# Router logits of a mixture-of-experts layer computed with tokens as rows instead of experts as rows

## Chip, cores and metric

The kernel runs on one core of one Trainium2 chip. The metric is the device time of one execution in microseconds (us), as the median of repeated runs. Beside it stands a profile of one execution: busy times, waits and the order of instructions on each engine (TensorE is PE, with its weight loads shown apart as PEld; VectorE is DVE, ScalarE is ACT, GpSimd is POOL, SyncE is SP, which issues the DMAs).

## What is computed

The input is 4 sequences of 1024 tokens with 128 features. Three layers with residual connections follow one another: a mixture of experts, a selective state-space layer (Mamba), and the same mixture of experts again.

```python
x = x + 0.5 * ffn(layernorm(x))
x = x + mamba(layernorm(x))
x = x + 0.5 * ffn(layernorm(x))

def ffn(x):                                   # 8 experts, all of them for all tokens
    router_probs = softmax(x @ w_router)      # [tokens, 8]
    gate_weights = softmax((x @ w_gating) / 0.1)
    h = silu(x @ w_gate[e]) * (x @ w_up[e])   # for each expert e, 128 -> 512
    expert_out[e] = h @ w_down[e]             # 512 -> 128
    cw = router_probs * gate_weights
    cw = cw / (cw.sum(-1) + 1e-9)
    return sum(expert_out[e] * cw[e])

def mamba(x):                                 # inner size 256, state size 16
    xs, z = split(x @ W_in)
    xc = silu(causal_conv4(xs) + conv_b)
    dt, B, C = split(xc @ W_x); dt = softplus(dt @ W_dt + b_dt)
    h_t = exp(dt_t * A) * h_(t-1) + dt_t * xc_t * B_t
    y_t = h_t . C_t + xc_t * D
    return (y * silu(z)) @ W_out
```

## The kernel before

**Blocks and stages.** The 4096 tokens are cut into 8 blocks of 512. `order` holds 16 mixture stages: (1, k) is the first mixture of block k, (2, k) the second. In between stands the Mamba part of each block. TensorE runs the stages one after another without a break: for each of the 8 experts of a stage, `gate_part` and `up_part` make two 128x1024 products each, and `down` brings the result back to 128 features. Everything else, the Mamba blocks among it, is threaded between these products.

**Splitting.** The wide products work on a high and a low part: a value is rounded to the faster type `float32r` (`xh`, `wh`) and the remainder is kept in a second tile (`xl`, `wl`). A product is then the sum of three: high x high, high x low, low x high (L641 to L643). The router weights are treated in the same way: `wrg` holds the 8 columns of `w_router` and the 8 of `w_gating`, 16 in all, padded with zeros to 128; `wrg_h` and `wrg_l` are its parts (L249 to L272).

**The plan.** All engines run in an order written out by the program. The class `Plan` holds a clock for each engine with assumed costs; work for VectorE is put in queues (`put`, with a cost and the time from which it is ready) and taken from them when its engine's assumed clock gets there (`fill`), or at once when something needs it (`need`). ScalarE's side work goes through `act_put` and `act_need`. An item's cost and time only decide its place in the order; on the chip each engine runs its instructions in that order and waits for what they read.

**Slots and events.** Time is counted in slots, 64 for each stage and 8 for each expert. A step such as `tr` or `logits` is an event with a slot and often a condition; `run_events` (L1152) lets a due event stand back while its condition says that its input isn't ready, for up to `wait` slots, 12 as a rule (`WAIT`), and then issues it anyhow. For the mixture stages the slots come from `WHEN` and `LOOSE`, counted from the start of the stage. For Mamba block k they count from `START[k]`, in three chains: `front` (norm, projections, convolution, softplus), `mid` (the 16 states, two at a time: exponentials on ScalarE, product, scans and read-out on VectorE, the sum on GpSimd) and `back` (`gate`, the product with silu(z), and `outproj`, the output projection L1073 and the residual). The chain `back` has a patience of 12 slots, and of 24 for the last block (L1177).

**One shared bank.** Small results in PSUM, TensorE's accumulators, go through a single bank, the tile `misc`: norm transposes, logits, projections and the end of each stage. Whoever wants it first waits until the reader of the one before is through (`plan.reader`).

**The logits.** For each stage, `tr` (L462) makes the transposed and split `xh` and `xl`, features as rows and the 512 tokens as columns. `logits` (L481) then makes three products with the padded router weights as the stationary side and all 512 tokens streamed past, which gives `lt`, logits as rows; ScalarE copies 16 rows of it to `ls` (L490), a tile of the ring `tmp` of three, shared with the copies of the expert results. `logits2` (L492), a second event, turns them back with four small transposes (L497) into `lg`, where tokens are rows and the 16 logits of each of the four groups of 128 tokens are columns. `shift` on VectorE takes the maximum of each softmax (L505) and subtracts it (L506). `burst` makes the exponentials on ScalarE, `cw1` to `cw3` the weights, and `cwt` transposes, stores and spreads them over all partitions by DMA.

Of the kernel before, what the change touches and what calls it, by code (L numbers as in the profile page):

```python
# [8 lines left out]
F32 = mybir.dt.float32  # L9
F32R = mybir.dt.float32r  # L10
AF = mybir.ActivationFunctionType
ALU = mybir.AluOpType
AX = mybir.AxisListType
# [5 lines left out]
BIG = 11  # L19
TMP = 3  # L20
TOL = 0.4
START = (72, 144, 232, 328, 432, 544, 656, 744)
REST = (4, 9, 17, 19, 23, 25, 29, 35, 37)
FRONT = {0: (5, 7, 8, 15, 16, 18, 21, 27, 29)}
ZT = {0: 11}
# [17 lines left out]
CWT0 = 11  # L43
# [5 lines left out]
NEVER = 1e9  # L49
WAIT = 12  # L50
# [122 lines left out]
def tile_macaron_mamba_moe(  # L173
# [20 lines left out]
    V, G, S, T = nc.vector, nc.gpsimd, nc.scalar, nc.tensor  # L194

    NB, L, H = x_in.shape
    E, _, F = w_gate.shape
# [3 lines left out]
    TB = 512  # L201
    J = TB // 128
    NBLK = NB * L // TB
# [3 lines left out]
    NE2 = 2 * E  # L207
    P = 128
# [4 lines left out]
    const = ctx.enter_context(tc.tile_pool(name="const", bufs=1))  # L213
    sb = ctx.enter_context(tc.tile_pool(name="sb", bufs=1))
# [3 lines left out]
    plan = Plan()  # L218
# [4 lines left out]
    def misc(name):  # L223
        if plan.reader in plan.spare:
            plan.act_need(plan.reader)
        plan.need(lambda: plan.reader is None or plan.reader[3])
        plan.wait_bank(name)
        return ps.tile([P, TB], F32, tag="misc", bufs=1, name=name)
# [17 lines left out]
    idle = ps.tile([P, P], F32, tag="pd", bufs=1, name="idle")  # L246
    for i in range(12):
        T.matmul(idle, blank, blank, start=True, stop=True)
    wrg = sb.tile([P, P], F32, tag="tmp", bufs=TMP, name="wrg")  # L249
    V.memset(wrg, 0.0)  # L250

    def load_router():
        nc.sync.dma_start(out=wrg[:, 0:E], in_=w_router)
# [2 lines left out]
    ident = const.tile([P, P], F32, name="ident")  # L256
# [7 lines left out]
    V.memset(over, -1.0 / H)  # L264
    V.memset(eps9, 1e-9)

    wrg_h = const.tile([P, P], F32R, name="wrg_h")
    wrg_l = const.tile([P, P], F32R, name="wrg_l")

    def split_router():  # L270
        V.tensor_copy(wrg_h, wrg)
        V.tensor_tensor(wrg_l, wrg, wrg_h.bitcast(F32), ALU.subtract)  # L272

    wh, wl, wd, raws, cast = {}, {}, {}, {}, {}

# [168 lines left out]
    def ffn_events(s):  # L444
        kind, k = order[s]
        d = ffn[s] = {}
        nm = f"f{kind}_{k}"
# [14 lines left out]
        def tr():  # L462
            pt, at = transposed(d["xn"], nm, plan.act_need(*d["xn_it"]))
            xh = d["xh"] = sb.tile([P, TB], F32R, tag="xh", bufs=2, name=f"xh_{nm}")
            xl = sb.tile([P, TB], F32R, tag="xl", bufs=2, name=f"xl_{nm}")
            S.copy(xh, pt)
            if s == 0:
                S.copy(wh[0][:, 1, :], raws[0][:, 1, :])

            def low():  # L470
                V.tensor_tensor(xl, pt, xh.bitcast(F32), ALU.subtract)
                d["xl"] = xl

            plan.reader = d["low"] = plan.put(low, 0.6, plan.on_act(0.6, at))
            if s == 0:
                plan.run(d["low"])
                split_router()
                raw = raws.pop(0)
                V.tensor_tensor(wl[0][:, 1, :], raw[:, 1, :], wh[0][:, 1, :].bitcast(F32), ALU.subtract)

        def logits():  # L481
            plan.need(lambda: "xl" in d)
            xh, xl = d["xh"], d["xl"]
            lt = misc(f"lt_{nm}")
            T.matmul(lt, wrg_h, xh, start=True, stop=False)
            T.matmul(lt, wrg_h, xl, start=False, stop=False)
            T.matmul(lt, wrg_l, xh, start=False, stop=True)
            ls = d["ls"] = sb.tile([NE2, TB], F32, tag="tmp", bufs=TMP, name=f"ls_{nm}")
            t = plan.on_pe(0.7, d["low"][4])
            plan.reader = d["ls_it"] = plan.act_put(lambda: S.copy(ls, lt[0:NE2, :]), 0.6, t)  # L490

        def logits2():  # L492
            ls = d["ls"]
            ls_at = plan.act_need(d["ls_it"])
            lg = misc(f"lg_{nm}")
            for j in range(J):
                T.transpose(  # L497
                    lg[:, j * NE2 : (j + 1) * NE2], ls[:, j * P : (j + 1) * P], ident[0:NE2, 0:NE2]
                )
            lv = lg[:, 0 : J * NE2].rearrange("p (j s e) -> p j s e", j=J, s=2)  # L500
            mx = sb.tile([P, J, 2], F32, tag="mx", bufs=2, name=f"mx_{nm}")
            ex = sb.tile([P, J, 2, E], F32, tag="ex", bufs=2, name=f"ex_{nm}")

            def shift():
                V.tensor_reduce(mx, lv, AX.X, ALU.max)  # L505
                V.tensor_tensor(  # L506
                    ex, lv, mx.unsqueeze(3).to_broadcast([P, J, 2, E]), ALU.subtract
                )
                d["ex"] = ex

            plan.reader = plan.put(shift, 0.3, plan.on_pe(0.3, ls_at))

        def burst(alone=True):
            if "exp" in d:
                return
            plan.need(lambda: "ex" in d)
            ex = d["ex"]
            S.activation(ex[:, :, 0, :], ex[:, :, 0, :], AF.Exp)
            S.activation(ex[:, :, 1, :], ex[:, :, 1, :], AF.Exp, scale=10.0)
            d["exp"] = ex  # L520
            if s == 1:
                a_neg()
            plan.put(cw1, 0.25, plan.on_act(0.3, 0.0, "exp"))
            if alone and (s == 1 or s > 13) and not plan.lo:
                S.preload_act_table_set("silu_and_others")
                plan.on_act(0.0, 0.0, "silu")
# [41 lines left out]

        free = plan.bank_free
        if s == 0:  # L570
            return [(0, ln), (0, nrm), (0, tr), (1, logits), (3, logits2), (4, burst), (CWT0, cwt, lambda: max(free(), d.get("cw_at", NEVER)))]
        ln_at, nrm_at, tr_at, lg_at, lg2_at, bu_at, cwt_at = WHEN.get(s, LOOSE)
        return [
            (ln_at - (8 if kind == 1 and s > 1 else 0), ln, lambda: 0.0 if kind == 1 or k in mixed else NEVER),
            (nrm_at, nrm, lambda: d.get("nb_at", NEVER)),
            (tr_at, tr, lambda: max(free(), max(i[4] or NEVER for i in d["xn_it"]))),
            (lg_at, logits, lambda: max(free(), d["low"][4] if d["low"][3] else NEVER)),
            (lg2_at, logits2, lambda: max(free(), d["ls_it"][4] or NEVER)),
            (lg2_at + 2, lambda: riders.append(lambda: burst(False)), lambda: 0.0 if "ex" in d else NEVER),
            (bu_at, burst, lambda: 0.0 if slot[0] % 8 == 5 and "ex" in d or "exp" in d else NEVER),  # L580
            (cwt_at, cwt, lambda: max(free(), d.get("cw_at", NEVER))),
# [567 lines left out]
    def add(base, evs, wait=WAIT):  # L1149
        chains.append([(max(0, base + ev[0]), wait, *ev[1:]) for ev in evs])  # L1150
# [15 lines left out]
    for s in range(len(order)):  # L1166
        add(8 * GPS * s, ffn_events(s))
        kind, k = order[s]
        if kind == 1 and k + 1 < NBLK:
            add(8 * GPS * s, [(0 if s == 0 else -12, lambda k=k: load_x(k + 1))])  # L1170
        if s < len(order) - 1:
            add(8 * GPS * (s + 1), [(FENDS.get(s, 16), lambda s=s: ffn_end(s), lambda s=s: max(plan.bank_free(), summed(s)))])
    for k in range(NBLK):
        front, mid, back = mamba_events(k)
        add(START[k], front)
        add(START[k], mid, 99)
        add(START[k], back, 24 if k == NBLK - 1 else WAIT)  # L1177
    for e in range(1, E):
        add(8 * (e - 1), [(WL, lambda e=e: load_expert(e)), (WS, lambda e=e: split_expert(e))])
    add(8 * E, [(-24, load_mamba)])  # L1180
# [59 lines left out]
```

## Time and profile before

| | |
|---|---|
| median of 3 runs | 1266.12 us (1266.01 to 1266.13) |
| the profiled execution | 1265.99 us |
| span of its instructions | 1264.2 us, 14417 instructions |
| TensorE's granted clock | 1.000 |
| L485 to L487, three wide logit products | 16 of each, 395 to 423 ns each in the record |
| L490, copy of the logits on ScalarE | x16, 9.0 us, 560 ns each |
| L497, transposes back | x64, 6.7 us, 213 ns each in the record |
| L505 and L506, maximum and difference on VectorE | x16 each, 215 and 224 ns each |

The span runs from the first to the last instruction of the program; the time of an execution also holds what lies before and behind it. Products on TensorE are pipelined and the ends in their records are modelled, so what one costs in a stream is read from the distance between two starts, not from its record. The chain of waits follows the last instruction back, at each step to what released it, and its shares say which engines set the end. A wait is put down to the instruction that came last.

### The profile page before, as it was taken

The numbers are of one execution on the slowest core, as the hardware profiler recorded it, in microseconds if no ns is written. First come the engines' busy times: TensorE is split into PE (matmuls) and PEld (weight loads), VectorE is DVE, ScalarE is ACT, GpSimd is POOL, SyncE is SP. The second block draws the span as 40 slices with busy tenths as digits, with TensorE's granted clock in tenths as the row PEclk, the third lists the DMA queues.
The fourth block names the chain that finished last, engine by engine and source line by source line (L and its number), as shares of the span: only waits on it lengthen the run. The fifth ranks groups of instructions, "written<-read, shape, count | busy, mean of one in ns | idle before, by whom it ended". The sixth has DMA issues, their size and how long they took to land.

```text
span 1264.2 us, 14417 instructions
## 1 busy us (share of the span) xinstructions
PE 1245.2 (99%) x4800; PEld 862.0 (68%) x4800; DVE 1138.2 (90%) x1286; ACT 921.8 (73%) x1326; POOL 706.1 (56%) x557
## 2 busy tenths in 40 slices
PE   9999999999999999999999999999999999999998
PEld 7776666666666666666666666666666666668787
DVE  6985699999899999999999999999999999998676
ACT  7684887776777768787788778778777776666653
POOL 1022465757568647775676567757775676554400
PEclk9999999999999999999999999999999999999999
DMA  4501333343343433334343353432433433311011
GB/s 147 158 26 34 107 112 86 101 112 82 81 107 97 118 91 95 93 99 110 99 100 96 92 119 84 120 98 82 113 98 79 110 92 109 103 56 42 26 43 25
DMA packets 75386, 115.09 MB, mean 91 GB/s; under 512 B 7472, under 2 KB 23728, under 8 KB 75312
## 3 DMA queue, kind: packets, MB, share of 16 engines
q1 hardware_dynamic: 75312, 114.19, 33.6%
q8 instruction: 37, 0.61, 0.2%
q14 instruction: 37, 0.30, 0.1%
HBM read 109.71 MB, written 4.46 MB: 90 GB/s over the span
## 4 chain that ended last, share of the span: by engine, by line
PE 70%; DVE 16%; ACT 5%; issue 5%; POOL 3%; DMA 1%; SPq 0%; DVEq 0%; ACTq 0%; POOLq 0%
PE pd L722 19%; PE pu L641 7%; PE pg L641 7%; PE pg L643 7%; PE pu L643 7%; PE pu L642 7%; PE pg L642 7%; DVE hb_m L1021 5%; DVE h L657 4%; PE pd L697 3%; DVE hb_m L1015 2%; DVE da_m L1033 2%; PE pd L705 1%; ACT da_m L1002 1%; ACT h L625 1%
## 5 line engine op out<-in xcount | busy, mean ns | idle before, releaser
L722 PE MATMUL pd<-h,wd 128*128 128x512 f32 x824 | 391.6, 592 | 1.2 <-ACT tmp L735 1.2
L657 DVE TENSOR_TENSOR h<-h,pu 128x1024 f32<-128x1024 f32 x256 | 311.1, 1215 | 76.9 <-PE pu L643 52.5
L1036 POOL TENSOR_TENSOR y_m<-y_m,da_m 128x1024 f32<-128x1024 f32 x128 | 310.5, 2426 | 106.5 <-DVE hb_m L1015 103.2
L625 ACT ACTIVATE h<-pg 128x1024 f32<-128x1024 f32 x256 | 262.7, 1026 | 140.2 <-PE pg L643 135.2
L641 PE MATMUL pg<-xh_f,wh 128*128 128x512 f32 x510 | 266.9, 523 | 0.7 <-ACT h L625 0.7
L744 POOL TENSOR_TENSOR tmp<-tmp,cwb 128x512 f32<-128x512 f32 x98 | 129.1, 1318 | 196.6 <-issue 106.2
L722 PEld LDWEIGHTS pd<-h,wd 128*128 128x128 f32 x824 | 153.5, 188 | 107.9 <-issue 89.6
L641 PE MATMUL pu<-xh_f,wh 128*128 128x512 f32 x512 | 205.8, 402 | 5.8 <-DVE h L657 5.6
L643 PE MATMUL pg<-xh_f,wl 128*128 128x512 f32 x510 | 201.1, 394 | 0.8 <-DVE wl L299 0.8
L643 PE MATMUL pu<-xh_f,wl 128*128 128x512 f32 x512 | 200.5, 392 | 0.0
L642 PE MATMUL pu<-xl_f,wh 128*128 128x512 f32 x512 | 199.9, 391 | 0.0
L642 PE MATMUL pg<-xl_f,wh 128*128 128x512 f32 x510 | 199.4, 391 | 0.0
L1015 DVE TENSOR_TENSOR hb_m<-dx_m,bcb_m 128x1024 f32<-128x1024 f32 x128 | 166.4, 1300 | 1.8
L1021 DVE TENSOR_TENSOR_SCAN hb_m<-da_m,st_sb,hb_m 128x512 f32<-128x512 f32 x128 | 164.2, 1283 | 2.3
L1002 ACT ACTIVATE da_m<-dt_m,A_sb 128x512 f32<-128x512 f32 x256 | 164.0, 711 | 0.6
L1021 DVE TENSOR_TENSOR_SCAN hb_m<-da_m,hb_m 128x512 f32<-128x512 f32 x128 | 156.7, 1224 | 2.6
L1033 DVE TENSOR_TENSOR da_m<-hb_m,bcb_m 128x1024 f32<-128x1024 f32 x128 | 155.8, 1217 | 1.5
L641 PEld LDWEIGHTS pg<-xh_f,wh 128*128 128x128 f32 x510 | 96.0, 188 | 64.8 <-issue 27.4
L747 POOL TENSOR_TENSOR acc<-acc,tmp 128x512 f32<-128x512 f32 x98 | 130.3, 1330 | 7.6
L642 PEld LDWEIGHTS pg<-xl_f,wh 128*128 128x128 f32 x510 | 96.3, 189 | 50.6 <-issue 36.5
L641 PEld LDWEIGHTS pu<-xh_f,wh 128*128 128x128 f32 x512 | 96.1, 188 | 35.4 <-DVE h L657 15.8
L643 PEld LDWEIGHTS pg<-xh_f,wl 128*128 128x128 f32 x510 | 95.6, 187 | 23.2 <-DVE wl L299 1.2
(181 smaller groups left out, 1494.7 us busy)
## 6 DMA issues: line engine op xcount, KB each, us to landing
bcb_m<-bc_m SPq DMA_DIRECT2D x128, 512.0 KB
cwb<-cd_f SPq DMA_DIRECT2D x128, 256.0 KB
out_dram<-x SPq DMA_DIRECT2D x13, 256.0 KB
x<-in_L_attn_x_dram SPq DMA_DIRECT2D x8, 256.0 KB
wraw<-in_L_ffn_w_gate_dram SPq DMA_DIRECT2D x8, 256.0 KB
wraw<-in_L_ffn_w_up_dram SPq DMA_DIRECT2D x8, 256.0 KB
wd<-in_L_ffn_w_down_dram SPq DMA_DIRECT2D x8, 256.0 KB
cd_f<-ct_f SPq DMA_DIRECT2D x64, 4.0 KB
```

Source lines behind the costliest of these rows:

```text
L625: S.activation(h, pg, AF.Silu)
L641: T.matmul(o[:, q, :], wh[e][:, i, cols[q]], d["xh"], start=True, stop=False)
L642: T.matmul(o[:, q, :], wh[e][:, i, cols[q]], d["xl"], start=False, stop=False)
L643: T.matmul(o[:, q, :], wl[e][:, i, cols[q]], d["xh"], start=False, stop=True)
L657: V.tensor_tensor(h, h, pu, ALU.mult)
L722: T.matmul(d["pd"], wd[e][:, cols], h[0], start=(f == 0), stop=(f == FC - 1))
L747: it = put(lambda: G_.tensor_tensor(acc, acc, t, ALU.add), 1.25, at)
L1002: S.activation(da[:, i, :], d["dt"][:, i, :], AF.Exp, scale=A_sb[:, i, n : n + 1])
L1015: mul = V.tensor_tensor(hb, d["dx"], bcb[:, 0:1, :].to_broadcast([P, ND, TB]), ALU.mult)
L1021: V.tensor_tensor_scan(hb[:, i, :], da[:, i, :], hb[:, i, :], 0.0 if first else st_sb[:, i, n : n + 1], ALU.mult, ALU.add,)
L1033: V.tensor_tensor(da, hb, bcb[:, 1:2, :].to_broadcast([P, ND, TB]), ALU.mult)
L1036: it = pool_put(lambda: G.tensor_tensor(d["y"], d["y"], da, ALU.add), 2.4, plan.dve)
```

## The change

The stationary side and the streamed side of the logits change places. For each of the four groups of 128 tokens, the slice of `xh` is the stationary side, and the high and low router weights stand side by side as 32 streamed columns, tile `wrg_s`; a second product with the slice of `xl` as the stationary side adds the high weights' 16 columns to the first half. The result has tokens as rows at once. The two halves are added by a reduction on VectorE, which replaces the first read of PSUM; the maximum and the difference then work on SBUF. The event `logits2`, the copy `ls` and the transposes are gone, as is the padding with zeros. The assumed costs are 0.88 on TensorE instead of 0.7 and 0.3, and 0.5 instead of 0.3 for `shift`. The start slots of Mamba blocks 4 to 7 are 8, 8, 16 and 16 earlier, and the chain `back` of every block has a patience of 40 slots.

```diff
--- before.py
+++ after.py
@@ -19,7 +19,7 @@
 BIG = 11
 TMP = 3
 TOL = 0.4
-START = (72, 144, 232, 328, 432, 544, 656, 744)
+START = (72, 144, 232, 328, 424, 536, 640, 728)
 REST = (4, 9, 17, 19, 23, 25, 29, 35, 37)
 FRONT = {0: (5, 7, 8, 15, 16, 18, 21, 27, 29)}
 ZT = {0: 11}
@@ -246,8 +246,7 @@
     idle = ps.tile([P, P], F32, tag="pd", bufs=1, name="idle")
     for i in range(12):
         T.matmul(idle, blank, blank, start=True, stop=True)
-    wrg = sb.tile([P, P], F32, tag="tmp", bufs=TMP, name="wrg")
-    V.memset(wrg, 0.0)
+    wrg = sb.tile([P, NE2], F32, tag="tmp", bufs=TMP, name="wrg")
 
     def load_router():
         nc.sync.dma_start(out=wrg[:, 0:E], in_=w_router)
@@ -264,12 +263,11 @@
     V.memset(over, -1.0 / H)
     V.memset(eps9, 1e-9)
 
-    wrg_h = const.tile([P, P], F32R, name="wrg_h")
-    wrg_l = const.tile([P, P], F32R, name="wrg_l")
+    wrg_s = const.tile([P, 2, NE2], F32R, name="wrg_s")
 
     def split_router():
-        V.tensor_copy(wrg_h, wrg)
-        V.tensor_tensor(wrg_l, wrg, wrg_h.bitcast(F32), ALU.subtract)
+        V.tensor_copy(wrg_s[:, 0, :], wrg)
+        V.tensor_tensor(wrg_s[:, 1, :], wrg, wrg_s[:, 0, :].bitcast(F32), ALU.subtract)
 
     wh, wl, wd, raws, cast = {}, {}, {}, {}, {}
 
@@ -482,33 +480,30 @@
             plan.need(lambda: "xl" in d)
             xh, xl = d["xh"], d["xl"]
             lt = misc(f"lt_{nm}")
-            T.matmul(lt, wrg_h, xh, start=True, stop=False)
-            T.matmul(lt, wrg_h, xl, start=False, stop=False)
-            T.matmul(lt, wrg_l, xh, start=False, stop=True)
-            ls = d["ls"] = sb.tile([NE2, TB], F32, tag="tmp", bufs=TMP, name=f"ls_{nm}")
-            t = plan.on_pe(0.7, d["low"][4])
-            plan.reader = d["ls_it"] = plan.act_put(lambda: S.copy(ls, lt[0:NE2, :]), 0.6, t)
-
-        def logits2():
-            ls = d["ls"]
-            ls_at = plan.act_need(d["ls_it"])
-            lg = misc(f"lg_{nm}")
+            lv = lt[:, 0 : 2 * J * NE2].rearrange("p (j h n) -> p j h n", j=J, h=2)
             for j in range(J):
-                T.transpose(
-                    lg[:, j * NE2 : (j + 1) * NE2], ls[:, j * P : (j + 1) * P], ident[0:NE2, 0:NE2]
+                T.matmul(
+                    lt[:, j * 2 * NE2 : (j + 1) * 2 * NE2], xh[:, j * P : (j + 1) * P],
+                    wrg_s.rearrange("p h n -> p (h n)"), start=True, stop=False,
                 )
-            lv = lg[:, 0 : J * NE2].rearrange("p (j s e) -> p j s e", j=J, s=2)
+                T.matmul(
+                    lt[:, j * 2 * NE2 : j * 2 * NE2 + NE2], xl[:, j * P : (j + 1) * P],
+                    wrg_s[:, 0, :], start=False, stop=True,
+                )
             mx = sb.tile([P, J, 2], F32, tag="mx", bufs=2, name=f"mx_{nm}")
             ex = sb.tile([P, J, 2, E], F32, tag="ex", bufs=2, name=f"ex_{nm}")
 
             def shift():
-                V.tensor_reduce(mx, lv, AX.X, ALU.max)
+                V.tensor_reduce(
+                    ex.rearrange("p j s e -> p j (s e)"), lv.rearrange("p j h n -> p j n h"), AX.X, ALU.add
+                )
+                V.tensor_reduce(mx, ex, AX.X, ALU.max)
                 V.tensor_tensor(
-                    ex, lv, mx.unsqueeze(3).to_broadcast([P, J, 2, E]), ALU.subtract
+                    ex, ex, mx.unsqueeze(3).to_broadcast([P, J, 2, E]), ALU.subtract
                 )
                 d["ex"] = ex
 
-            plan.reader = plan.put(shift, 0.3, plan.on_pe(0.3, ls_at))
+            plan.reader = plan.put(shift, 0.5, plan.on_pe(0.88, d["low"][4]))
 
         def burst(alone=True):
             if "exp" in d:
@@ -568,14 +563,13 @@
 
         free = plan.bank_free
         if s == 0:
-            return [(0, ln), (0, nrm), (0, tr), (1, logits), (3, logits2), (4, burst), (CWT0, cwt, lambda: max(free(), d.get("cw_at", NEVER)))]
+            return [(0, ln), (0, nrm), (0, tr), (1, logits), (4, burst), (CWT0, cwt, lambda: max(free(), d.get("cw_at", NEVER)))]
         ln_at, nrm_at, tr_at, lg_at, lg2_at, bu_at, cwt_at = WHEN.get(s, LOOSE)
         return [
             (ln_at - (8 if kind == 1 and s > 1 else 0), ln, lambda: 0.0 if kind == 1 or k in mixed else NEVER),
             (nrm_at, nrm, lambda: d.get("nb_at", NEVER)),
             (tr_at, tr, lambda: max(free(), max(i[4] or NEVER for i in d["xn_it"]))),
             (lg_at, logits, lambda: max(free(), d["low"][4] if d["low"][3] else NEVER)),
-            (lg2_at, logits2, lambda: max(free(), d["ls_it"][4] or NEVER)),
             (lg2_at + 2, lambda: riders.append(lambda: burst(False)), lambda: 0.0 if "ex" in d else NEVER),
             (bu_at, burst, lambda: 0.0 if slot[0] % 8 == 5 and "ex" in d or "exp" in d else NEVER),
             (cwt_at, cwt, lambda: max(free(), d.get("cw_at", NEVER))),
@@ -1174,7 +1168,7 @@
         front, mid, back = mamba_events(k)
         add(START[k], front)
         add(START[k], mid, 99)
-        add(START[k], back, 24 if k == NBLK - 1 else WAIT)
+        add(START[k], back, 40)
     for e in range(1, E):
         add(8 * (e - 1), [(WL, lambda e=e: load_expert(e)), (WS, lambda e=e: split_expert(e))])
     add(8 * E, [(-24, load_mamba)])
```

## The prediction

> **What bounds the kernel.** I read the page's busy rows and slices first, then the chain of waits, then the waits of TensorE, then the order in time around single logits, and last the groups of instructions with the shapes kept apart.
>
> ```profile
> PE 1245.2 (99%) x4800; PEld 862.0 (68%) x4800; DVE 1138.2 (90%) x1286; ACT 921.8 (73%) x1326; POOL 706.1 (56%) x557
> ...
> PE   9999999999999999999999999999999999999998
> ...
> DVE  6985699999899999999999999999999999998676
> ...
> PE 70%; DVE 16%; ACT 5%; issue 5%; POOL 3%; DMA 1%; SPq 0%; DVEq 0%; ACTq 0%; POOLq 0%
> ```
>
> TensorE is full in all slices but the last, and 70% of the chain that ends last runs through it. A busy PE row alone does not prove that it works at its rate, so I compared starts: in the quiet stretches of the three-product lines (L641 to L643) one 128x512 product follows another after 0.227 us, and the largest groups add up to roughly 1215 us at their own quiet spacing. What is left, about 45 us, is the head (the first product starts at 8.36 us), the tail, and waits. So time taken from TensorE's stream comes off the end nearly one for one. VectorE is the second engine: in the middle stages it stands at 76 or 77 us of 80, with some 3 to 5 us free in each. That its delays do reach TensorE is seen in the waits (columns: us in total, times, longest us):
>
> ```profile
> PE pu L641 <- DVE h L657: 5.6, 11, 0.9
> ...
> PE lt_f L485 <- DVE xl_f L471: 0.8, 2, 0.6
> ...
> PE cwt_f L556 <- POOL cw_f L547: 0.5, 1, 0.5
> ```
>
> **What goes from TensorE.** The logits run 16 times. The three wide products start at 9.86, 10.09 and 10.33 us, and the next line's at 10.56: 0.70 us. The four transposes back are worth a look in the order in time (columns: start, us, engine, line):
>
> ```profile
> 778.02 0.40 PE L643 MATMUL pg<-xh_f,wl 128*128 128x512 f32 x1
> 778.35 0.42 PE L497 MATMUL lg_f<-ident,ls_f 16*128 16x16 f32 x4
> 778.70 0.50 PE L641 MATMUL pu<-xh_f,wh 128*128 128x512 f32 x1
> 779.04 0.40 PE L642 MATMUL pu<-xl_f,wh 128*128 128x512 f32 x1
> ```
>
> From L643 to L642 there are 1.02 us where two ordinary steps would take 0.45, so four transposes of 16 columns cost 0.56 us, with hardly any streaming in them. The product behind them shows 0.50 instead of 0.39: its own weight load, otherwise hidden under the product before, lies open for 0.11. I read 0.56 as five open loads of 0.112, the four of the transposes and the next one. All 16 places give 0.55 to 0.56. Removed: 16 x (0.70 + 0.56) = 20.2 us.
>
> **What comes to TensorE.** Eight pairs of a full 128x128 load (a slice of xh or xl) and a product of 32 or 16 columns. No row shows this form, so bounds: the output projection L1073 runs 16 pairs with full loads in 1.78 us, 0.111 each, giving 0.89; the transposes at 0.56 / 4 = 0.14 a pair give 1.12. Farther off, the load's record is 0.188 long (L485); eight of them one after another would be 1.50, though the open part just seen speaks against it. The transposes are nearest, for they too have nothing to stream under which a load could hide; by their reading I take nine open loads, 9 x 0.112 = 1.01, or 16.1 us in all. Net for TensorE: -4.0 us, with -6.0 (0.89) and -2.3 (1.12) as near ends and +3.9 (1.50) as the far one.
>
> A rule of the Trainium skill speaks against the change: the page "TensorEngine Tiling (Array Packing)", section "When to Use Tiling", would make a streamed side of 64 columns or fewer the stationary one, and here the narrow side becomes the streamed one. The page "TensorE: Matmul & The Clock Gate", section "LDWEIGHTS (loading the stationary operand)", gives columns / 1.2 ns, so by an estimate from it eight loads take 0.85 us and the net would be -6.5 us; the open 0.11 in the trace agrees with that rate, and the first rule overlooks that the narrow stationary form brings transposes with it.
>
> **VectorE.** Three operations instead of two on its in-order queue, ahead of whatever up-product (L657) is behind them; TensorE waits for that through pu. Removed: 0.215 (L505) + 0.224 (L506) = 0.439. Added: a sum over 128 elements. The reduces over 32 and 64 take 0.178 (L540) and 0.212 (L533), 0.034 per 32, so 128 make 0.28; then the maximum from SBUF like L533, 0.212, and the difference, 0.22. Together 0.71, or +0.27 each, +4.4 us in all. The bounds on the path are 0 (the free 3 to 5 us of each stage hide it) and 4.4 (no cover left); I take its share of the chain, 16%, +0.7 us.
>
> **ScalarE and the shared bank.** The copy L490 goes, 16 x 0.56 = 9.0 us of an engine with a quarter free; at its 5% of the chain, -0.4. The single misc bank is taken once instead of twice; of the waits that name it, 0.2 us of L890 on ex and 1.0 us of loads on ls, the loads are partly under products. Bounds for both together are 0 and -1.2; I keep -0.4 and add nothing. The tmp ring of three loses a user, which only loosens it.
>
> **Head.** The memset (0.165) and the split over 128 columns (0.217 + 0.292) shrink to 16 columns. After the split VectorE makes wl, done at 10.10 and first read by L643 at 11.03: 0.9 us of cover, so I book nothing; uncovered it would be at most -0.5. The two DMAs of the router stay in place on SP's queue, and their landing is before the split either way.
>
> **Starts and patience.** A stage of 64 slots takes about 80 us, so 8 and 16 slots are 10 and 20 us: blocks 4 and 5, then 6 and 7, issue everything earlier, their norms, projections, the bc store and its reload on SP's queue, scans, gate and output projection. The scans cannot move that far: their read-outs (L1033) run nearly without a gap from 274 to 1102 us, VectorE being their limit. What does move is the gate and projection at a fixed offset; block 7's read-out ends at 1102 and its projection starts only at 1153, so there is room. The longer wait of 40 slots lets a projection stand back when its product is late; one such stall is seen, 0.43 us beyond the ordinary step in front of L1073 at 404.3, for GpSimd's gate product L1062. I book -0.4 for it and 0 for the earlier starts, with ends of -1.3 (the L485 and L556 waits shown above vanish) and +5.6 (the waits for the up-product double because VectorE's queue is kept fuller).
>
> **Sum.** -4.0 + 0.7 - 0.4 - 0.4 = -4.1 us. The profiled execution took 1265.99 us with a span of 1264.2, 1.8 us lying around it; the median is 1266.12, so the offset is the same: 1262.0 us.
>
> **Rivals.**
> - *Larger gain, 1258.0.* Loads at the L1073 price (-6.0), ScalarE and the projection as above (-0.8), VectorE's extra hidden, both late waits gone (-1.3): -8.1. For it: load and stream overlap there. Against it: that row streams 128 columns to hide under. Chance 0.14.
> - *Nothing that can be measured, 1265.5.* TensorE comes to the up-products sooner and waits there: of the -4.1, 3.5 return as waits on L657 (it already has 5.6). For it: VectorE above 95% in the middle. Against it: 70% of the chain is TensorE. A measurement tells apart about 0.2%, 2.5 us. Chance 0.16.
> - *Slower through VectorE, 1271.3.* Blocks 4 to 7 pressed closer and 4.4 us more reduces use up its free time; up-products come late. All 4.4 on the path, the 5.6 doubled, less 4.0 and 0.8: +5.2. It decides once a middle stage has less free than the 0.27 added plus one displaced 1.2 us operation, against 3 to 5 now. Chance 0.13.
> - *Slower through the loads, 1269.9.* Open loads of 0.188: +3.9 + 0.7 - 0.8 = +3.8. Decides above 0.157 a pair, where eight equal the 1.26 removed. Chance 0.05.
>
> **How the numbers follow.** The forecast has 0.52, its own range 1259.3 to 1263.7 (the -6.0 end with VectorE's part hidden, and the -2.3 end). Faster by over 0.2%: 0.52 + 0.14 = 0.66; within: 0.16; slower: 0.13 + 0.05, 0.18. The range 1257.0 to 1269.0 leaves out the tips of the larger gain and much of the slower cases.
>
> **What would show it.** Eight products of 32 and 16 columns spaced near 0.11 us; the span from the product before to the second after near 1.01 above two steps (0.89 and 1.12 are the ends, 1.50 the fourth rival). A sum of 0.28 us on VectorE, L490 and L497 gone. TensorE's wait on L657 at about 5.6; above 10 the third rival is at work. The projection at 404 without its stall. The forecast is wrong if TensorE's stream is shorter by 4 us and the span is not: then the waits tell where it went.

## The result, and the profile after

The changed kernel is slower: 1274.11 us in the median of 4 runs (1273.98 to 1276.78) against 1266.07 us for the kernel before on the same chip. The ratio is 1.0068, with a 95% interval of 1.0053 to 1.0082, so 8.0 us are lost where 4.1 were forecast to be won. The profiled execution of after is the longest of its four, 1276.78 us with a span of 1274.7; its granted clock is 0.997 because two stretches of 3.4 us, from 8.2 and from 605.5 us, ran at half clock, by estimate some 1.7 us each. The execution of after with a granted clock of 1.000 took 1273.98 us, so the loss of 8.0 us does not need them. The profile is read for places and durations, and the sums below are made from medians, in which a difference of a microsecond can be the clock's.

The busy row, two rows of slices and the chain of the page after:

```profile
PE 1245.5 (98%) x4816; PEld 862.3 (68%) x4816; DVE 1142.6 (90%) x1301; ACT 908.7 (71%) x1306; POOL 703.5 (55%) x557
...
PE   9999999999999999999999999999999999999998
...
DVE  5985599999999999999989999999998999998676
...
PE 14%; DVE 3%; issue 1%; POOL 1%; ACT 0%; DVEq 0%; POOLq 0%
```

TensorE is as busy as before in the record (1245.2) although it has less to do: the record of a product that is held up or runs at half clock is longer, as a row below shows, so the busy row does not show the saving. The chain's shares add up to 19% only: it was followed back through the last fifth of the span and lost there, so it can't be set beside the 70% of before. What helps is the list of TensorE's waits (us in total, times, longest):

```profile
PE pu L635 <- DVE h L651: 7.3, 14, 1.4
PE pg L635 <- ACT h L619: 3.9, 5, 1.4
PE pd L699 <- DVE hl L661: 3.3, 2, 1.7
PE lt_f L485 <- DVE xl_f L469: 1.8, 2, 1.2
PE cwt_f L551 <- POOL cw_f L542: 1.4, 2, 0.9
```

Every one has grown: the up-products' (L635 after L651) from 5.6, the gate products' (L635 after L619) from 0.7, the down-products' (L699) from 1.7, the logits' from 0.8, the transposes' of the weights from 0.5. No single one is as large as the loss, and they lie all over the span. The groups that belong to the change, shapes kept apart (us busy, mean ns of one, idle before):

```profile
L489 PE MATMUL lt_f<-wrg_s,xl_f 128*128 128x16 f32 x64 | 15.0, 258 | 0.0
L485 PE MATMUL lt_f<-wrg_s,xh_f 128*128 128x32 f32 x64 | 14.2, 251 | 2.1 <-DVE xl_f L469 1.8 <-DVE st_sb L1026 0.3
...
L501 DVE TENSOR_TENSOR ex_f<-ex_f,mx_f 128x64 f32<-128x64 f32 x16 | 8.3, 521 | 0.5
L497 DVE TENSOR_REDUCE ex_f<-lt_f 128x64 f32<-128x128 f32 x16 | 4.5, 283 | 3.8 <-PE lt_f L489 3.8
L500 DVE TENSOR_REDUCE mx_f<-ex_f 128x8 f32<-128x64 f32 x16 | 3.5, 220 | 0.6
```

The sum over 128 elements takes 283 ns and the maximum 220, as forecast. The difference does not: 521 ns where L506 took 224. And the new products are cheaper than forecast. Their distances are seen in the order in time (start, us, engine, line; the wait ahead in brackets):

```profile
603.34 0.28 PE L485 MATMUL lt_f<-wrg_s,xh_f 128*128 128x32 f32 x1 [1.19 <-DVE xl_f L469]
603.47 0.26 PE L489 MATMUL lt_f<-wrg_s,xl_f 128*128 128x16 f32 x1
603.58 0.26 PE L485 MATMUL lt_f<-wrg_s,xh_f 128*128 128x32 f32 x1
...
604.14 0.26 PE L489 MATMUL lt_f<-wrg_s,xl_f 128*128 128x16 f32 x1
604.25 0.48 PE L635 MATMUL pu<-xh_f,wh 128*128 128x512 f32 x1
...
605.91 3.37 PE L716 MATMUL pd<-h,wd 128*128 128x512 f32 x4
```

From 603.34 to 604.25 there are 0.91 us for eight pairs: 0.112 each after the first. Measured as the prediction measured the old ones, from the product before to the second after, less two ordinary steps, 10 of the 16 places cost 0.89 to 0.90 us. So TensorE's work went down by 16 times some 0.36 us, about 5.7 us. The last row shows something else: four down-products that take 3.37 us here take 1.88 us elsewhere. The granted clock of the stretch says why (length, then busy us of PE, PEld, DVE, ACT, POOL with counts, granted clock, share of DMA, GB/s):

```profile
606.00:610.00 4.00, 4.00 (x8) 1.55 (x7) 3.83 (x7) 1.08 (x2) 0.57 (x1) 0.64 0.45 113
```

**Where TensorE falls behind.** For every product I took its start less the sum of the quiet steps of all products ahead of it, which is what TensorE has lost so far, and cut each kernel's stream at the same shares of its work. The growth of that loss in us, in profiled executions, by stretches that end near the time named, with some kernels of the experiments below (the last row is e8 of experiment 4):

```
                          300   450   600   750   900  1050  1200   end
before                   15.3   4.2   3.1   4.9   3.9   5.5   4.5   1.1
after                    18.8   5.8   7.4   4.3   7.8   7.1   5.4   1.2
early starts, old logits 16.7   4.2   4.4   7.3  16.5   4.1   3.2   1.2
blocks 4 and 6 earlier   17.0   4.2   4.3   5.6  11.3   3.2   5.9   1.1
blocks 4, 5, 7 earlier   16.8   4.2   4.3   7.3   3.6   3.9  12.0   1.2
new logits, old order    15.5   5.4   3.1   5.7   3.5   5.8   3.9   1.2
```

Before loses 42.5 us in all, after 57.8. The 15.3 more eat the 5.7 won and leave 9.6 of the 10.5 us by which the two profiled spans differ; the other 0.9 lie behind the start of the last product. By estimate up to 3.4 of the 15.3 are the two stretches at half clock. The rest comes in most stretches, so one cause would not do; the experiments take the change apart.

### The profile page after: what moved, and what is told of

Same layout as the page of the kernel before. It is cut to its first block, busy times and chain, and to the rows that moved or that the text cites. A ratio compares the mean times of both kernels' runs of the same rounds, so it can differ in the third digit from the quotient of the medians.

```text
span 1274.7 us, 14444 instructions
## 1 busy us (share of the span) xinstructions
PE 1245.5 (98%) x4816; PEld 862.3 (68%) x4816; DVE 1142.6 (90%) x1301; ACT 908.7 (71%) x1306; POOL 703.5 (55%) x557
## 5 line engine op out<-in xcount | busy, mean ns | idle before, releaser
L651 DVE TENSOR_TENSOR h<-h,pu 128x1024 f32<-128x1024 f32 x256 | 310.8, 1214 | 77.3 <-PE pu L637 53.0
L619 ACT ACTIVATE h<-pg 128x1024 f32<-128x1024 f32 x256 | 262.6, 1026 | 158.3 <-PE pg L637 151.8
L635 PE MATMUL pg<-xh_f,wh 128*128 128x512 f32 x510 | 263.9, 518 | 4.6 <-ACT h L619 3.9
L738 POOL TENSOR_TENSOR tmp<-tmp,cwb 128x512 f32<-128x512 f32 x98 | 131.8, 1345 | 201.7 <-issue 85.1
L635 PE MATMUL pu<-xh_f,wh 128*128 128x512 f32 x512 | 207.1, 404 | 7.8 <-DVE h L651 7.3
L635 PEld LDWEIGHTS pg<-xh_f,wh 128*128 128x128 f32 x510 | 96.0, 188 | 72.0 <-issue 27.3
L635 PEld LDWEIGHTS pu<-xh_f,wh 128*128 128x128 f32 x512 | 96.2, 188 | 39.4 <-DVE h L651 19.8
```

The source lines that it names most:

```text
L619: S.activation(h, pg, AF.Silu)
L635: T.matmul(o[:, q, :], wh[e][:, i, cols[q]], d["xh"], start=True, stop=False)
L651: V.tensor_tensor(h, h, pu, ALU.mult)
L738: it = put(lambda: G_.tensor_tensor(t, t, cwb, ALU.mult), 1.25, at)
```

## The experiments

The kernel before was run with each group: 1266.24, 1265.99, 1266.17 and 1266.15 us. Ratios are to the kernel before in the same group, with the 95% interval; they take in all executions and so differ a little from the quotient of the medians.

**1. The early starts alone.** The logits of before, `START` and patience of the change.

```diff
-START = (72, 144, 232, 328, 432, 544, 656, 744)
+START = (72, 144, 232, 328, 424, 536, 640, 728)
-        add(START[k], back, 24 if k == NBLK - 1 else WAIT)
+        add(START[k], back, 40)
```

> The old logits, with only the earlier starts of blocks 4 to 7 and the patience of 40 slots. Three theories. ORDER: the time goes to a different order of all the work around the logits, which the plan makes from other assumed costs, and not to the logits themselves; then this, which is a reordering too, may land anywhere from 1264 to 1271, with no tie to the 1274 of the change. VECTOR: the added reduction and the slower difference on VectorE make the up-products late; then this has none of it, 1265 to 1267. MOVES: the earlier starts crowd VectorE and ScalarE; then 1271 to 1275 here.

Measured: 1278.97 us, 1.0096 (1.0081 to 1.0112): 12.7 us lost by a part that was booked at nothing. With the old logits the patience moves no instruction, so this is the starts' doing. The profiled execution is the slowest of the four (1281.06 us, granted clock 0.994), 15.1 us above that of before, and the table above puts 12.6 of these between 750 and 900 us, where block 6 begins (slot 640 of 64 slots in 80 us is 800 us). The order in time there:

```profile
818.12 0.69 DVE L806 TENSOR_TENSOR x<-x,fo 128x512 f32<-128x512 f32 x1 [0.54 <-PE fo L798]
...
822.38 0.20 POOL L360 TENSOR_TENSOR nb_m<-nb_m,minus 128x4 f32<-128x4 f32 x1
...
822.61 0.49 ACT L414 ACTIVATE xn_m<-x,nb_m,rs_m 128x128 f32<-128x128 f32 x1 [0.79 <-POOL nb_m L360]
...
824.04 1.28 ACT L1002 ACT_TABLE_LOAD   x1
...
825.33 2.56 ACT L1002 ACTIVATE da_m<-dt_m,A_sb 128x512 f32<-128x512 f32 x4
825.52 0.27 PE L438 MATMUL pt_m<-ident,xn_m 128*128 128x128 f32 x1
...
827.80 1.25 ACT L414 ACTIVATE xn_m<-x,nb_m,rs_m 128x128 f32<-128x128 f32 x3
...
828.33 0.86 PE L438 MATMUL pt_m<-ident,xn_m 128*128 128x128 f32 x2 [2.54 <-ACT xn_m L414]
```

The first mixture of block 6 hands over `x` at 818.12. Its norm for the Mamba block needs VectorE, GpSimd (until 822.58) and ScalarE. ScalarE makes one of four groups of tokens, and then, as its written order has it, a silu, a table load and four exponentials of another block. TensorE has been sent to the transposes at 825.52, does the one that it can, and stands for 2.54 us. The transposes were due while the norm was not done; they are issued after their 12 slots of patience all the same. From 827.8 us, still within the wait, the clock is halved for nearly 7 us:

```profile
826.00:830.00 4.00, 1.67 (x5) 1.17 (x6) 3.90 (x4) 3.44 (x8) 2.54 (x4) 0.73 0.25 51
830.00:834.00 4.00, 4.00 (x11) 3.11 (x10) 3.34 (x4) 2.50 (x3) 1.53 (x1) 0.50 0.35 80
834.00:838.00 4.00, 4.00 (x14) 2.57 (x13) 3.16 (x3) 0.71 (x2) 0.00 (x0) 0.92 0.61 172
```

So a wait of 2.5 us costs about 6, by estimate: itself, and half of 6.8 us at half clock. Two more waits follow in this stretch, 0.97 us at 868.18 (L954, for `xc_m`) and 2.66 us at 878.18 (L975, for `dt_m` on ScalarE), and from 879.0 another 3.4 us at half clock; together that makes some 11 of the 12.6 us. The execution with the highest granted clock, 0.998, still took 1276.89 us, so most of the loss does not need the half clock. The Trainium skill, "TensorE: Matmul & The Clock Gate", section "Part 1: The HAM clock gate (the "warmup" mystery)", has the clock at half rate after at least one idle window of 3.4 us. The lengths seen here, 3.4 and 6.8 us, fit its window. Its rule on when does not: here waits of only 1.2 us (603.34, after) and 2.5 us went ahead of it. The length of a wait does not decide either: a10 (experiment 5) has the same wait of 1.19 us at 600.37 and m46 (experiment 2) one of 2.57 us at 1145.58, both with the clock at 1.00 behind them, and of two nearly equal waits, 1.81 us at 380.83 in e4 (experiment 3) and 1.80 us at 383.03 in e5 (experiment 4), only the second is followed by half clock. What decides stays open; that a wait causes it at all is read from the order of the two and was not tried by itself.

**2. Which blocks.** Two kernels with the old logits and some of the earlier starts, and one with the changed logits (sum left in PSUM, see 4) in which blocks 4 and 7 go back:

```diff
 m46:  START = (72, 144, 232, 328, 424, 544, 640, 744)
 m457: START = (72, 144, 232, 328, 424, 536, 656, 728)
 a11:  START = (72, 144, 232, 328, 432, 536, 640, 744)
```

> The old logits, with blocks 4 and 6 started earlier, 5 and 7 left. BLOCK 6: 1274 to 1280. CROWDING: half of the 12.7 us, 1270 to 1274.

> The old logits, with blocks 4, 5 and 7 started earlier and block 6 left at 656. BLOCK 6 (its norm is now due at slot 637, before slot 649 where the mixture that feeds it hands over, so its steps are issued before their inputs are there): 1265 to 1269. CROWDING (all earlier starts together fill VectorE and ScalarE): 1272 to 1277, some two thirds or more of the 12.7 us of all four.

> The changed kernel with the sum written back to PSUM and the starts of blocks 4 and 7 back at 432 and 744 (blocks 5 and 6 stay earlier; without one of these the plan can't be made). BLOCK 6: it stays, so little is won against 1271.9, 1270 to 1274. CROWDING: 1265 to 1269.

Measured: 1275.68 us (1.0070, 1.0055 to 1.0085), 1276.75 (1.0083, 1.0068 to 1.0098) and 1275.66 (1.0070, 1.0055 to 1.0086). The idea that block 6 alone was too early fell: without it the time is hardly better. The loss only moves: m46 has its 11.3 us at 750 to 900, m457 none there but 12.0 between 1050 and 1200, where block 7's projection meets a gate product that isn't made:

```profile
1150.89 1.07 PE L697 MATMUL pd<-hh,wds 128*128 128x512 f32 x4
1154.48 2.56 PE L1073 MATMUL po_m<-w_out_sb,zs_m 128*128 128x128 f32 x16 [2.52 <-DVE zs_m L1057]
```

The projection takes 2.56 us in the record instead of 2.05: the clock is halved there again (0.59 in the stretch from 1156 to 1160). In before the same steps of block 7, the last read-out, GpSimd's sum, the gate product and the projection, stand so:

```profile
1144.87 1.22 DVE L1033 TENSOR_TENSOR da_m<-hb_m,bcb_m 128x1024 f32<-128x1024 f32 x1
...
1147.45 2.40 POOL L1036 TENSOR_TENSOR y_m<-y_m,da_m 128x1024 f32<-128x1024 f32 x1
...
1151.98 1.21 DVE L1057 TENSOR_TENSOR zs_m<-zs_m,y_m 128x1024 f32<-128x1024 f32 x1
...
1153.25 2.05 PE L1073 MATMUL po_m<-w_out_sb,zs_m 128*128 128x128 f32 x16
```

The projection starts 0.06 us after the gate product ends, and that 7 us after the last read-out, so it can come 16 slots, 20 us, earlier only if the read-outs do. In m457 they do not: the last one starts at 1147.00. In e1, with all four blocks earlier, it starts at 1131.68, and the projection at 1142.42 has no wait. And a11, with two blocks less moved than the same kernel with the full change of starts (a10 in 5, 1271.93), is 3.7 us slower than it, though two of its four executions have a granted clock of 0.994. The starts do not add up block by block.

**3. VectorE's share without the new products.** The old logits in the old order, with a sum-like reduction over 128 elements put ahead (each element taken twice, so the values stay) and the difference made from SBUF:

```diff
-                V.tensor_reduce(mx, lv, AX.X, ALU.max)
+                V.tensor_reduce(
+                    ex.rearrange("p j s e -> p j (s e)"),
+                    lg[:, 0 : J * NE2].rearrange("p (j n) -> p j n", j=J).unsqueeze(3).to_broadcast([P, J, NE2, 2]),
+                    AX.X, ALU.max,
+                )
+                V.tensor_reduce(mx, ex, AX.X, ALU.max)
...
-                    ex, lv, mx.unsqueeze(3).to_broadcast([P, J, 2, E]), ALU.subtract
+                    ex, ex, mx.unsqueeze(3).to_broadcast([P, J, 2, E]), ALU.subtract
```

> The old logits in the old order, but VectorE makes three operations as in the change: a reduction of 128 elements from PSUM (here the maximum of each value with itself), the maximum from SBUF, and the difference with both sides in SBUF, all at the old assumed cost. VECTOR: most of the loss is here, 1270 to 1275. ORDER and MOVES: hidden for the most part, 1266 to 1268.

Measured: 1272.26 us, 1.0051 (1.0034 to 1.0068): 6.0 lost where +0.7 was booked. Two views of it, its group of the difference and TensorE's wait for the up-products, 5.6 us before:

```profile
L511 DVE TENSOR_TENSOR ex_f<-ex_f,mx_f 128x64 f32<-128x64 f32 x16 | 10.8, 673 | 0.5
```

```profile
PE pu L646 <- DVE h L662: 10.2, 14, 1.8
```

The difference took 224 ns from PSUM and takes 673 from SBUF. Why is seen in the order in time of after, where one of them is caught:

```profile
454.14 2.36 POOL L1030 TENSOR_TENSOR y_m<-y_m,da_m 128x1024 f32<-128x1024 f32 x1 [6.86 <-DVE hb_m L1009]
454.55 2.04 DVE L501 TENSOR_TENSOR ex_f<-ex_f,mx_f 128x64 f32<-128x64 f32 x1
...
456.51 1.21 DVE L651 TENSOR_TENSOR h<-h,pu 128x1024 f32<-128x1024 f32 x1
```

An operation of 0.22 us begins 0.41 us after a long addition on GpSimd and ends at 456.59, 0.09 us after that addition. In after 6 of the 16 are stretched so, to 0.44 to 2.04 us, and all six end 0.08 to 0.09 us after a GpSimd operation that had begun before them; the shortest take 0.22. The Trainium skill, "SBUF — State Buffer", section "Who interferes with whom", says that a VectorE instruction with two SBUF inputs and a GpSimd instruction that reads SBUF take one read interface in turn, the later one waiting for the whole of the other. The trace agrees, 2.04 us for 0.22; the prediction did not use it.

**4. The new products in the old order.** Here the new products stand where the transposes were, an empty item keeps the place of the copy in the plan, and all other instructions keep their order. e5 has the change's `shift`; e8 writes the sum back into free columns of the PSUM tile, so that the difference reads PSUM; e6 leaves out the maximum and the difference (the exponentials of the unshifted logits, whose common factor cancels in the quotient).

```diff
 e8 and a10, in shift():
+                sv = lt[:, 2 * J * NE2 : 3 * J * NE2].rearrange("p (j n) -> p j n", j=J)
+                V.tensor_reduce(sv, lv.rearrange("p j h n -> p j n h"), AX.X, ALU.add)
+                hv = sv.rearrange("p j (s e) -> p j s e", s=2)
+                V.tensor_reduce(mx, hv, AX.X, ALU.max)
...
-                    ex, ex, mx.unsqueeze(3).to_broadcast([P, J, 2, E]), ALU.subtract
+                    ex, hv, mx.unsqueeze(3).to_broadcast([P, J, 2, E]), ALU.subtract
```

> The new logits with every assumed cost, event and start of the old kernel, so that all other instructions on all engines stand in the old order; the eight pairs stand where the transposes back stood. ORDER: TensorE's stream is 5.7 us shorter and nothing is shuffled, so 1260 to 1263. VECTOR: the three operations on VectorE cost as much here as in the change, so 1270 to 1275. MOVES: 1260 to 1264.

> The new logits in the old order, but the sum of the two halves is written back to PSUM, so that maximum and difference read PSUM as in the old kernel; still three operations. PORT (the difference with both sides in SBUF waits for GpSimd's long operations, up to 2.1 us a time): 3 to 5 us below the 1268.2 of the new logits in the old order, 1263 to 1265. REDUCTION (any third operation on VectorE costs this much): 1267 to 1269.

> The new logits in the old order, without the maximum and the difference (the factor they stand for cancels in the quotient): one operation on VectorE instead of two in the old kernel. If TensorE's shorter stream (5.7 us) reaches the end when VectorE is not burdened: 1259 to 1262. If TensorE's saving is lost to other waits in any case: 1265 to 1268.

Measured: e5 1268.21 us (1.0015, 1.0005 to 1.0025), e8 1262.43 (0.9976, 0.9964 to 0.9987), e6 1259.07 (0.9943, 0.9928 to 0.9958). The one difference between e5 and e8, the place of the sum, is worth 5.8 us, and 4.8 between their executions at a granted clock of 0.999 or more (1266.96 and 1262.20 in the median). In e8 the difference is back at its length, though 7 of its 16 run beside a GpSimd operation, and the up-products' wait is near that of before:

```profile
L510 DVE TENSOR_TENSOR ex_f<-lt_f,mx_f 128x64 f32<-128x64 f32 x16 | 3.6, 224 | 0.5
```

```profile
PE pu L645 <- DVE h L661: 6.5, 11, 1.3
```

These runs also price VectorE's time. From e8 to e6 it loses 0.289 + 0.224 + 0.224 - 0.279 = 0.458 us a stage, 7.3 in all, and the end comes 3.4 us sooner: 0.46 us for one. From before to e4 it gains 0.282 + 0.220 + 0.673 - 0.439 = 0.736 a stage, 11.8 in all, and the end is 6.0 later: 0.51 for one. Half, not the 16% of the chain. With it e8 is accounted for: -5.7 on TensorE, and 4.8 us more VectorE time at 0.46, +2.2, make -3.5; measured -3.6.

**5. The change with one part undone.** a10 is the change with the sum in PSUM; e2b is the change with the old patience.

> The changed kernel with the sum written back to PSUM, order otherwise as in the change. PORT: 3 to 5 us below 1274.1, 1269 to 1271, and what is left above 1266 is the order with its earlier starts. ORDER alone: 1273 to 1275.

> The changed kernel with the old patience of the chain back (12 slots, 24 for the last block), the earlier starts kept. MOVES, if by the patience: 1265 to 1269. ORDER: another order, 1269 to 1277. VECTOR: as the change, 1273 to 1275.

Measured: a10 1271.93 us (1.0045, 1.0030 to 1.0060), 2.2 below after; e2b 1277.37 (1.0083, 1.0068 to 1.0098), 3.3 above it, and 1.6 above it between the executions at a granted clock of 1.000 (1275.62 and 1273.98). So the patience helps here, by more than was booked. Whether it mends a loss by the early starts was not tried by itself: with the old logits it moves nothing, early starts or not. Even with the sum in PSUM the change is slower than before, so the wait for GpSimd is the smaller part.

**6. The order alone.** The kernel before with one assumed cost changed, 0.5 for `shift` instead of 0.3, which moves instructions in VectorE's order (at least 175 of 1286, by the two traces) and adds no work; and e8 with the same edit.

```diff
-            plan.reader = plan.put(shift, 0.3, plan.on_pe(0.3, ls_at))
+            plan.reader = plan.put(shift, 0.5, plan.on_pe(0.3, ls_at))
```

> The old kernel with nothing changed but one assumed cost in the plan, 0.5 instead of 0.3 for the maximum and difference; the instructions are the same, some hundred stand elsewhere. ORDER: a reordering costs by itself, 1268 to 1275. If the order matters only through the earlier starts: 1265.5 to 1267.5.

> The new logits with the sum in PSUM, in the order that the old kernel takes with an assumed cost of 0.5 for the maximum and difference. If the gains of the two add up: 1262.4 - 1.1, some 1261. If the order's gain belongs to the old instructions: 1262 to 1265.

Measured: n1 1264.88 us (0.9992, 0.9982 to 1.0001) and e8n 1262.16 (0.9966, 0.9955 to 0.9977). Such an edit is worth some 1.1 us in the median with no work changed, though the interval reaches 1, and what it brings to one kernel it does not bring to the next: e8n is within its spread of e8.

**7. The change's own events with the old starts.** In e8 the copy's place was kept. The change makes the logits one event instead of two, and the plan sets all that follows anew. With the change's assumed costs and the old starts the planner finds no order (a norm falls due ahead of the Mamba block it needs), so these four have others. All but p6 have the sum in PSUM.

```diff
 p3 (old starts, old patience), p4 (starts and patience of the change), p6 (as p3, shift as in the change):
-            plan.reader = plan.put(shift, 0.5, plan.on_pe(0.88, d["low"][4]))
+            plan.reader = plan.put(shift, 0.3, plan.on_pe(1.0, d["low"][4]))
 p5 (as p3):
+            plan.reader = plan.put(shift, 0.25, plan.on_pe(0.88, d["low"][4]))
```

> The new logits as one event as in the change, sum in PSUM, but the old starts and the old patience, with 1.0 and 0.3 as assumed costs so that the plan can be made. STARTS (the earlier starts are what the order costs): 1261 to 1265. REST (leaving out the second event and the copy shuffles the order to its harm): 1269 to 1273.

> The same with the early starts and the patience of the change. STARTS: 6 to 12 us above the run with old starts, 1270 to 1276. REST: within 2 us of it.

> Old starts and patience again, with 0.88 and 0.25 as assumed costs, so another order of the same work. STARTS: 1260 to 1266, like the first. If orders differ much among themselves whatever the starts: more than 3 us from the first.

> The logits exactly as in the change, sum and difference in SBUF, with the old starts and patience and 1.0 and 0.3 as assumed costs. If the difference waits for GpSimd here as elsewhere: 2 to 6 us above the run with the sum in PSUM. If the loss of the change is all in the starts: at most 1 us above it.

Measured: p3 1266.89 us (1.0003, 0.9993 to 1.0012), p4 1275.88 (1.0073, 1.0058 to 1.0088), p5 1266.41 (1.0003, 0.9993 to 1.0012), p6 1269.91 (1.0030, 1.0019 to 1.0041). From p3 to p4 only starts and patience differ: 9.0 us. From p3 to p6 only the place of the sum: 3.0. And p3 and p5 agree, some 4 us above e8, but their orders are nearly one: 21 of VectorE's 1301 instructions have to be moved to turn one into the other, against 203 from p3 to e8. So this order around the logits gives back the whole gain of the new products, even without the two other losses. Whether one event instead of two does so as such, or this order is a bad one by chance, was not tried: p4 and a10 differ in nothing but two assumed costs and lie some 4 us apart.

Where the early starts cost time in the changed kernel is seen in the gate products' wait for ScalarE: 0.7 us in p3, 2.5 in p4, 3.8 in a10 and 3.9 in after. The longest in after stands behind four exponentials of a Mamba block:

```profile
881.24 2.56 ACT L996 ACTIVATE da_m<-dt_m,A_sb 128x512 f32<-128x512 f32 x4
...
885.11 1.02 ACT L619 ACTIVATE h<-pg 128x1024 f32<-128x1024 f32 x1
...
886.19 0.50 PE L635 MATMUL pg<-xh_f,wh 128*128 128x512 f32 x1 [1.38 <-ACT h L619]
```

The two waits of experiments 1 and 2 are not met in after: block 6's transposes at 826.26 and block 7's projection at 1163.26 start without one.

**The account.** Nine of the sixteen times (e1, e5, e8, a10, e2b, a11, n1, p3 and p5) fell outside every range expected for them; in e5 and a10 losses that were set against each other as rivals are there together. In medians, from before (1266.1) to after (1274.1):

```
new products, old order, sum in PSUM        1262.4   -3.7
the change's own event and order (p3)       1266.9   +4.5
its starts, patience, assumed costs (a10)   1271.9   +5.0
the difference from SBUF (after)            1274.1   +2.2
```

The steps depend on the order in which they are taken: the starts cost 5.0, 9.0 (p3 to p4) or 12.7 us (e1), the place of the sum 2.2, 3.0 (p6) or 5.8 (e5). Their signs hold in all of them. Between executions at a granted clock of 0.999 or more the four steps are -3.8, +3.8, +5.2 and +2.9 us.

## Why the prediction was wrong

- **TensorE, -4.0 booked, -5.7 measured.** The mechanism and both bounds were right, the choice between them was not. The transposes were taken as the nearest row, with one open load more than there are pairs (1.01 us). The L1073 price, 0.111 a pair, was the right one (0.90 measured): the row with the same full load priced the pair, though it streams 128 columns and not 32 or 16. The fourth rival, with open loads of 0.188, is out.
- **VectorE, +0.7 booked.** Two durations were right to 0.01 us. Two things failed. "I take its share of the chain, 16%": half of what VectorE is given reaches the end (0.46 and 0.51). And "the difference, 0.22" was taken from a row that reads PSUM, though the text says that the new ones work from SBUF. There it waits for GpSimd, 0.52 on average and up to 2.04. By the measured price the 4.4 us alone are +2.2, and the stretching (8.3 - 3.6 us) another 2.3, which agrees with the 2.2 between a10 and after.
- **The early starts, 0 booked, end +5.6.** This is the step with the largest miss: 5 to 13 us. The prediction let the gate and the projection move because "block 7's read-out ends at 1102 and its projection starts only at 1153, so there is room". That is a misreading: in before the last read-out of block 7 ends at 1146.09 and its gate product at 1153.19 (experiment 2), so the projection already started as soon as it could, and could move only with the read-outs. Nor did the prediction ask when the inputs of the other moved steps exist. Their slots run out first: at the norm of block 6 (experiment 1) and the gate product of block 7 (experiment 2) TensorE stands for 2.5 us, where the longest such wait that the prediction found in before was 0.43 us (L1073 at 404 us). These two waits are seen with the old logits (e1, m457). In after the same starts show as gate products that wait for ScalarE, 3.9 us instead of 0.7; the rest of the starts' share there was not traced to single waits. That a late input can be followed by half clock was not seen coming, and no row of before shows it; after loses its 8 us without it, too.
- **Patience, -0.4 booked.** The stall that it was booked for is still there: in after TensorE sits idle for 0.25 us ahead of the same projection at 407.03, in before for 0.27. With the old logits the patience moves nothing; with the change it is worth 3.3 us (1.6 at full clock), in another place.
- **ScalarE, -0.4 booked.** The copies are gone, 9.0 us, and ScalarE's busy time fell by 13.1. A gain of its own was not isolated: e8's sum closes without it.
- **What had no step at all.** One event instead of two changes the plan's clock, and with it the order of work far from the logits, +4.5 us in the one order that was run. The prediction held only the work of an edit against the time, not the new order that the planner writes for the rest. Which of the exchanged instructions matter stays open: p3's loss over e8 lies in several stretches, +2.9 us before 600 and +2.6 before 900 among them, and other stretches win.
- **The rivals.** The third, slower through VectorE at 1271.3, had the sign, and its sentence "Blocks 4 to 7 pressed closer and 4.4 us more reduces" names two of the parts. Its price was built on the up-products' wait doubling, 5.6 to 11; it went to 7.3, and the rest came in the waits of gate products, down-products, logits and weight transposes. That five waits would each grow a little was no case of its own.

## What to carry to other kernels

In a kernel whose whole order is written by a planner, price an edit in three parts: the work, the waits of what is moved (for each moved step, when its last input exists), and the new order of everything else. The last cost 4.5 us here, about as much as the work saved, and is measured by holding the old order and changing the work alone. Where an operand of VectorE goes from PSUM to SBUF, look at what GpSimd does at that time: 0.22 us became up to 2.04. And read from the trace when the last input of a step ends before giving it room. The fastest version is e6, the new products in the old order without the maximum: 1259.07 us, for inputs small enough that the exponentials need no shift; with the maximum it is e8 at 1262.43.

## What the runs showed of the hardware

- Eight pairs of a full 128x128 load and a product of 32 or 16 columns follow one another at 0.112 us, nearly the same as with 128 columns (0.111, L1073 before): from 16 to 128 streamed columns the stream does not set the pace.
- A small VectorE operation with both inputs in SBUF was held until a GpSimd operation that had begun before it ended: 16 of them took 10.8 us instead of 3.6 in e4, and 11.0 in p6. With one input in PSUM all 16 took 0.22 us in e8, 7 of them beside a GpSimd operation.
- TensorE's granted clock fell to a half for 3.4 us, or twice that, near waits of only 1.2 to 2.7 us: at 605.5 us in after, 827.8 and 879.0 in e1, 1155.8 in m457. Waits of the same lengths passed without it, 1.19 us in a10, 1.81 in e4 and 2.57 in m46; the profiled executions of before, e4, e8 and a10 show no such stretch between their start and their last microseconds.
